# Where the quantised tiles of x are made: beside other stages instead of inside the w2 loops

## The chip, the cores and the metric

The kernel runs on one core of one Trainium2 chip. Its engines are TensorE (PE, with weight loads shown as PEld), VectorE (DVE), ScalarE (ACT), GpSimd (POOL) and SyncE (SP, which here only issues DMAs). Each engine works off its own list of instructions in order and waits where an operand or a buffer is not ready. The metric is the device time of one execution in microseconds.

## The reference

Two layers over x of shape 2 x 4096 x 512, all in float32. What matters here:

```python
xn = _layernorm(x)
x1 = xn @ w1_w.T + w1_b                      # layer 0, "attention": a state-space model
x_conv = _silu(_depthwise_conv(x1, conv_w))  # three taps over the tokens
x_ssm = _ssm(x_conv, A, B_ssm, C_ssm, D_ssm) # a recurrence along 4096 tokens
v = _silu(xn @ v1_w.T + v1_b)
attn = x_ssm * v @ w2_w.T + w2_b
xq, xs = _mx_quantize(xn)                    # layer 0, "ffn": blocks of 32 channels,
wq, ws = _mx_quantize(weight)                # each value to the nearest point of a 6-bit grid
ffn = (xq * xs) @ (wq * ws).T + bias
x = x + attn + ffn
xn = _layernorm(x)                           # layer 1
q, k, v = relu(xn @ Wq.T + bq), relu(xn @ Wk.T + bk), xn @ Wv.T + bv
ctx = (q @ (k^T v)) / (q . sum(k))           # linear attention, 16 heads
y = _layernorm(ctx + xn) * gamma + beta
r, k2 = sigmoid(xr @ W_r.T), square(relu(xk @ W_k.T))   # xr, xk: mixed with the token before
x = x + y + r * (k2 @ W_v.T)
```

`_mx_quantize` takes the largest magnitude of each 32 channels, scales by it and rounds. It needs nothing but the normalised input: it depends on no other part of layer 0.

## The kernel before

The two batches of 4096 tokens are cut into 8 blocks of 512 tokens each (16 blocks, `NK`), and a block into 4 tiles of 128 tokens by 512 channels (`TJ`). The stages follow each other on PE, with the profile's times of each:

- 0 to 451 us, the projections by w1 and v1 of all 16 blocks (`projected`, and `projected_pair` for blocks 13 and 14, with seven products of quarters in place of eight). A block takes 27.5 us. DVE applies the taps (L468), turns the result (L477) and turns the normalised input of the next block into `xnT` (`turned`, L333, two buffers); ACT normalises (L136) and empties the banks (L364, L379).
- 451 to 560 us, the recurrence.
- For batch 0: the w2 loop (`mixed`, 560 to 877 us), the outer sums k^T x (`outer_sums`, 877 to 988), q and W_k by pairs of blocks (`pairs`, 988 to 1192) and the rest of layer 1 (`layer1`, 1192 to 1440).
- For batch 1 the same: 1440 to 1747, 1747 to 1858, 1858 to 2057 and 2057 to 2310 us.

One tile is quantised by `quantised` (L447 to L461), a generator with four steps. It issues the load of the tile from `xi`, the input laid out by blocks of 32 channels (L450, on SP); ACT normalises it in four instructions (L136), DVE finds the largest magnitudes (L187), scales them (L188) and inverts them (L192), and POOL multiplies (L193); DVE rounds (L201) and POOL multiplies back (L202); DVE transposes the tile to its place (L458). The place is a slice of a buffer in SBUF, or a temporary `mx_c` (one buffer), from which SP writes it to `xqd` in DRAM (L460).

Within the w2 loop, block i's product by w2 and by the quantised weight is `x1_by_seven`: DVE makes sums of quarters (L758), PE does seven products (L776), and DVE adds each into x (L794). The first bank is used again by the second product into it, so PE waits for L794. Between products, `gate` prepares the next block's gated input: two loads on SP, a transpose (L621) and a product with v (L622) on DVE. After it comes the product x by Wk of the block before with the key sum on POOL (L848). `tick` is called at fixed points of the loop, and `at` hangs work on a tick: the reading back of x1 (`turned_x1`) and the steps of the tiles to be quantised (L653 to L657), two ticks from tile to tile, four ticks for a tile.

Where the tiles are made before the change: those of blocks 3 to 7 of each batch within its own w2 loop (20 tiles each); blocks 0, 1 and 2 of batch 0 beside the projections, by the table `beside` (L1305); blocks 0 and 1 of batch 1 in `pairs` of batch 0 (`at_pair`, 2 tiles a pair, steps at the start and the middle of a pair) and block 2 in `layer1` of batch 0 (`at_block`). Block 2 of both batches and block 1 of batch 1 go through `xqd` and are read back by `xd_read`, 1 MB each.

In `pairs`, each of the two times seven products of a pair empties its banks by `put_q` (DVE add L1101, ACT L1102) or `put_k` (L1110, then ACT L1111 and L1112), 16 calls a pair; `hold` (L1072, ACT) copies products that are added to later ones; `token_sums` (L1046, DVE) makes the sums `ts` for the next half, `mixed_k` (L1127, L1128) and `mixed_r` (L1137, L1138) the mixed inputs. In `outer_sums`, ACT rescales four tiles of x1 per block, POOL makes the sums `sx` (L927) and DVE the sums `sk` (L935) for the block's seven products on PE (L955); the sums' generator yields once after a block's sums and once after each product.

The order of the instructions on each engine is fixed when the kernel is built: a scheduler places each where its operands and buffers are expected to be ready, and it keeps close to the order in which the program names them.

Of the kernel before, what the change touches and what calls it, by code (L numbers as in the profile page):

```python
# [10 lines left out]
F32 = mybir.dt.float32  # L11
# [6 lines left out]
P = 128  # L18
# [26 lines left out]
def block_kernel(ctx: ExitStack, tc: tile.TileContext, a: dict, out: bass.AP):  # L45
# [400 lines left out]

    def quantised(n, j, dst, temp):  # L447

        xq = yv.tile([P, D], F32, tag="yv", name="xq")
        nc.sync.dma_start(out=xq, in_=a["xi"][n * TJ + j])  # L450
        yield
        laid_normalised(xq, mvi[:, :, n, j, :])
        scales = mx_scaled(xq)
        yield
        mx_rounded(xq, scales)
        yield
        xd = dst().rearrange("p c t -> p (c t)") if dst else temp()
        nc.vector.transpose(xd, xq)  # L458
        if not dst:
            nc.sync.dma_start(out=xqd[n, j], in_=xd)  # L460
        yield  # L461

    def tapped(work, n, x1, cc):
# [160 lines left out]
    def mixed(b, z0, xds, xnTs, mvs, w2, wk, outer):  # L624

        ksum = stay.tile([P, D], F32, tag="ksum", name="ksum", bufs=1)
        zs, xts, pos = {0: z0}, {}, {}
        ahead = len(xds)
        plain = 2 if b == 0 else 1

        def xd_of(m, j):
            if m not in xds:
                xds[m] = t8((P, TJ, CC, P))
            return xds[m][:, j]

# [14 lines left out]
        def at(time, do):  # L650
            events[max(time, clock[0])].append(do)

        for m in range(ahead, NB):  # L653
            for j in range(TJ):
                q = quantised(b * NB + m, j, partial(xd_of, m, j), t2q)
                for step in range(4):
                    at(2 * TJ * (m - 2) + 2 * j - 6 + step, partial(next, q))  # L657

# [191 lines left out]

        if xds[1] is None:
            xd_read(1)
# [12 lines left out]
        for i in range(NB):  # L865
# [13 lines left out]
            if i == 0:  # L879
                first_x1_turned([xn[:, j, :] for j in range(TJ)])  # L880
            xnT = xnTs[i]
            for j in range(TJ):
# [210 lines left out]

    def pairs(b, xnTs, wq, wk, made, kvx, at_pair):

        xks = {}

        def put_q(p, o, n, pm, addend):
            t = t2("q")
            if addend is not None:  # L1100
                nc.vector.tensor_tensor(t, pm, addend, ALU.add)  # L1101
# [12 lines left out]

        def of_q(p):
# [31 lines left out]
        for p in range(NP):  # L1147
            at_pair(p, 0)

# [10 lines left out]
            mixed_r(p)  # L1160
            at_pair(p, 1)

# [83 lines left out]
    with tc.tile_pool(name="tab", bufs=1) as tab:  # L1246
# [3 lines left out]
        with pool("a", 2) as work, pool("pm", 1) as pm:  # L1250
# [46 lines left out]
            def quantise(m, j, dst):  # L1297
# [8 lines left out]
                1: [(0, 0)], 2: [(0, 1)], 3: [(0, 2)], 4: [(0, 3)], 5: [(2, 0)],  # L1306
                9: [(1, 0)], 10: [(1, 1)], 11: [(1, 2)],
                12: [("w", 0), ("w", 1), (1, 3)],
                13: [("w", 2), ("w", 3), (2, 1)],
                14: [(2, 2), (2, 3)],  # L1310
            }
            xd_b1 = None

            def beside_block(n):
                nonlocal xd_b1
                for what, j in beside.get(n, ()):
# [4 lines left out]
                    elif what == 1:  # L1321
                        if xd_b1 is None:
                            xd_b1 = by_tile(single.tile([P, CC * (T + 1)], F32, name="wide"))
                        quantise(1, j, lambda: xd_b1[:, j])
                    else:
                        quantise(2, j, None)

# [61 lines left out]
    for cc in range(CC):  # L1389
        gated(0, 0, z0, cc)  # L1390
    xds = {0: xd0, 1: xd_b1, 2: None}

    for b in range(B):
# [16 lines left out]

        def at_pair(p, half):

            if b + 1 < B:
                for m in range(2):
                    for _ in range(2):
                        next(ahead[m][p])
# [10 lines left out]

        next_in = []
        pairs(b, xnTs, wq, wk1, made, kvx, at_pair)
        layer1(b, xnTs, mvs, kvx, [load_weight(s) for s in ("W_r", "W_v")], at_block)  # L1430
        if b + 1 < B:
            z0, xds = next_in[0], {0: xd0, 1: None, 2: None}
            c_wts = [load_weight("w2_w"), load_weight("Wk")]
# [63 lines left out]
```

## Time and profile before

| | us |
|---|---|
| time, median of 3 runs (lowest, highest) | 2316.46 (2315.31, 2316.96) |
| the profiled execution's own time | 2312.19 |
| its span | 2310.4 |
| PE busy in the span | 2256.2 |
| DVE, ACT, POOL busy | 1615.7, 1024.3, 546.4 |
| HBM traffic | 378.65 MB |

The profile is of one execution. A row of a group names the line, the engine, the operation, output and input, shapes and count; behind the first bar stand the busy time in us and the mean of one in ns, behind the second the engine's idle time just before these instructions and what ended it. A row of waits gives who waited at which line for whom, then us in all, how often, and the longest. In the table by stretches, each engine has its busy time in the stretch and the number of its instructions; PE's granted clock stands as a share of full speed.

### The profile page before, as it was taken

The numbers are of one execution on the slowest core, as the hardware profiler recorded it, in microseconds if no ns is written. First come the engines' busy times: TensorE is split into PE (matmuls) and PEld (weight loads), VectorE is DVE, ScalarE is ACT, GpSimd is POOL, SyncE is SP. The second block draws the span as 40 slices with busy tenths as digits, with TensorE's granted clock in tenths as the row PEclk, the third lists the DMA queues.
The fourth block names the chain that finished last, engine by engine and source line by source line (L and its number), as shares of the span: only waits on it lengthen the run. The fifth ranks groups of instructions, "written<-read, shape, count | busy, mean of one in ns | idle before, by whom it ended". The sixth has DMA issues, their size and how long they took to land. (4 is left out here: it accounts for less than half of the span.)

```text
span 2310.4 us, 24818 instructions
## 1 busy us (share of the span) xinstructions
PE 2256.2 (98%) x7648; PEld 1268.4 (55%) x7648; DVE 1615.7 (70%) x3147; ACT 1024.3 (44%) x2019; POOL 546.4 (24%) x550
## 2 busy tenths in 40 slices
PE   7999999999999899999999999999999999999999
PEld 3444444455476676854445554667676854445554
DVE  6788676665788864376758779688964365667777
ACT  5787674454242333357752222234233246642222
POOL 0011200011445435500021112345434500001111
PEclk9999999999999999999999999999999999999999
DMA  7854542589664556412284435455557312253431
GB/s 249 290 166 139 154 148 108 164 273 330 213 201 153 158 189 209 132 69 110 96 291 155 145 117 185 145 166 190 174 169 223 128 51 96 86 209 146 146 125 58
DMA packets 280725, 378.65 MB, mean 164 GB/s; under 512 B 58256, under 2 KB 119696, under 8 KB 279568
## 3 DMA queue, kind: packets, MB, share of 16 engines
q1 hardware_dynamic: 251504, 309.94, 41.0%
q10 hardware_dynamic: 29088, 67.12, 7.5%
q8 instruction: 61, 1.00, 0.2%
q14 instruction: 72, 0.59, 0.1%
HBM read 238.93 MB, written 138.04 MB: 163 GB/s over the span
## 5 line engine op out<-in xcount | busy, mean ns | idle before, releaser
L1214 POOL TENSOR_TENSOR x<-x,row_beta 128x512 f32<-128x512 f32 x64 | 83.9, 1311 | 591.8 <-ACT xn L136 591.8
L165 PE MATMUL p_acc<-w_W_v,t 128*128 128x512 f32 x512 | 222.3, 592 | 0.0
L165 PE MATMUL p_acc<-w_W_r,xnT 128*128 128x512 f32 x448 | 201.4, 592 | 0.0
L193 POOL TENSOR_TENSOR xq<-xq,mx_rs 128x512 f32<-128x512 f32 x64 | 70.1, 1102 | 404.0 <-DVE mx_rs L192 244.9
L165 PEld LDWEIGHTS p_acc<-w_W_v,t 128*128 128x128 f32 x512 | 97.3, 190 | 122.5 <-issue 119.3
L1220 ACT ACTIVATE r<-p_acc 128x512 f32<-128x512 f32 x64 | 38.2, 597 | 260.6 <-PE p_acc L165 246.5
L136 ACT ACTIVATE xq<-xq,mvi 128x128 f32<-128x128 f32 x256 | 105.9, 483 | 89.1 <-DMA xq<-in_xi 82.5
L848 POOL TENSOR_TENSOR ksum<-ksum,k 128x512 f32<-128x512 f32 x62 | 82.9, 1336 | 205.3 <-ACT k L888 205.2
L776 PE MATMUL p_mm<-w_sums,t 128*128 128x256 f32 x416 | 101.8, 401 | 29.4 <-DVE x L794 29.4
L888 ACT ACTIVATE k<-k 128x512 f32<-128x512 f32 x64 | 40.3, 630 | 202.7 <-DVE k L887 182.4
L468 DVE SCALAR_TENSOR_TENSOR xc<-x,col_conv_w,xc 128x512 f32<-128x512 f32 x128 | 98.1, 787 | 40.0 <-ACT xc L466 21.8
L165 PEld LDWEIGHTS p_acc<-w_W_r,xnT 128*128 128x128 f32 x448 | 80.8, 190 | 80.4 <-issue 80.4
L776 PEld LDWEIGHTS p_mm<-w_sums,t 128*128 128x128 f32 x416 | 83.0, 202 | 45.6 <-DVE x L794 33.5
L165 PE MATMUL p_acc<-xnT,w_w_w 128*128 128x512 f32 x224 | 102.8, 602 | 2.4 <-DVE xnT L333 1.7
L165 PE MATMUL p_acc<-w_Wk,xnT 128*128 128x512 f32 x224 | 100.7, 592 | 0.0
L165 PE MATMUL p_acc<-xnT,w_v_w 128*128 128x512 f32 x224 | 100.7, 592 | 0.0
L165 PE MATMUL p_tr<-w_Wk,xnT 128*128 128x512 f32 x224 | 100.7, 592 | 0.0
L131 DVE BATCH_NORM_STATS2 st<-x 128x6 f32<-128x512 f32 x128 | 84.1, 678 | 22.7 <-DMA x<-in_x 22.0
L1234 DVE TENSOR_TENSOR r<-r,p_acc 128x512 f32<-128x512 f32 x64 | 43.9, 685 | 75.9 <-PE p_acc L165 75.9
L136 ACT ACTIVATE xi<-xi,mvi 128x128 f32<-128x128 f32 x208 | 89.3, 483 | 15.0 <-DMA xi<-in_xi 7.5
L118 ACT ACTIVATE rs_s<-rs_v 128x4 f32<-128x4 f32 (+1 forms) x41 | 8.4, 206 | 196.7 <-DVE rs_v L116 196.6
L776 PE MATMUL p_acc<-w_sums,t 128*128 128x256 f32 x416 | 94.0, 379 | 0.0
(294 smaller groups left out, 4981.8 us busy)
## 6 DMA issues: line engine op xcount, KB each, us to landing
x<-in_x SPq DMA_DIRECT2D x126, 256.0 KB, 5.3
xq<-in_xi SPq DMA_DIRECT2D x64, 256.0 KB, 4.6
vd<-v ACTq DMA_DIRECT2D x64, 256.0 KB, 2.5
cd<-xs SPq DMA_DIRECT2D x64, 256.0 KB, 2.0
xg<-cd SPq DMA_DIRECT2D x16, 1024.0 KB, 7.9
v<-vd SPq DMA_DIRECT2D x64, 256.0 KB, 4.5
xd<-x SPq DMA_DIRECT2D x64, 256.0 KB, 2.3
ktd<-k SPq DMA_DIRECT2D x64, 256.0 KB, 2.2
```

What stands on the lines that cost most here:

```text
L118: nc.scalar.activation(s, v, AF.Sqrt)
L131: nc.vector.bn_stats(st[:, j, :], xt(j))
L136: nc.scalar.activation(dst, src, AF.Identity, bias=mv[:, 0:1], scale=mv[:, 1:2])
L165: nc.tensor.matmul(out_ap, lhsT=lhsT(k), rhs=rhs(k), start=(k == 0), stop=(k == CC - 1))
L193: nc.gpsimd.tensor_tensor(by_block(y), by_block(y), rs.unsqueeze(2).to_broadcast([P, NQ, QB]), ALU.mult)
L468: nc.vector.scalar_tensor_tensor(xc, x1[:, tap : tap + T], conv_w[:, cc, tap : tap + 1], xc, ALU.mult, ALU.add,)
L776: nc.tensor.matmul(po[:, u * 2 * P : (u + 1) * 2 * P], lhsT=x(k)[:, c, u, :], rhs=w(k)[:, c, :], start=first and k == 0 and c == 0 and u == 0,
L848: nc.gpsimd.tensor_tensor(ksum, ksum, kt, ALU.add)
L888: nc.scalar.activation(kt, kt, AF.Relu)
L1214: nc.gpsimd.tensor_tensor(xt[j], xt[j], beta, ALU.add)
L1220: nc.scalar.activation(r, pr, AF.Sigmoid)
L1234: nc.vector.tensor_tensor(rs[j], rs[j], pf, ALU.mult)
```

## The change

All 28 tiles of blocks 1 to 7 of batch 1 and the 24 of blocks 2 to 7 of batch 0 are made outside the w2 loops, written to `xqd`, and read back by `xd_read`, 1 MB per block, two blocks ahead of use, at the start of the product by Wk. Their new places:

- batch 0: blocks 3 to 7 beside blocks 7 to 15 of the projections, in the table `beside`; blocks 0 and 1 stay in SBUF as before;
- batch 1: blocks 6 and 7 in the outer sums of batch 0 (`early`, a step at every second item of the generator, with the tile loaded into a buffer of the pool `t2`), blocks 1 to 5 in the pairs of batch 0 (`later`, a call of `stepped` after each `put_q` and `put_k`), block 0 in `layer1` of batch 0.

`stepped` keeps two tiles under way: each call does the next step of the first, and once that one has done three of its four steps, of the second too, so that a tile takes two calls.

```diff
-    def quantised(n, j, dst, temp):
+    def quantised(n, j, dst, temp, home=None):
-        xq = yv.tile([P, D], F32, tag="yv", name="xq")
+        xq = home("xq") if home else yv.tile([P, D], F32, tag="yv", name="xq")
...
+    done = {}
+
+    def stepped(tiles):
+
+        for tile_steps in tiles[:2]:
+            if tile_steps is tiles[0] or done.get(tiles[0], 0) > 2:
+                next(tile_steps)
+                done[tile_steps] = done.get(tile_steps, 0) + 1
+        while tiles and done.get(tiles[0]) == 4:
+            tiles.pop(0)
...
-        for m in range(ahead, NB):
-            for j in range(TJ):
-                q = quantised(b * NB + m, j, partial(xd_of, m, j), t2q)
-                for step in range(4):
-                    at(2 * TJ * (m - 2) + 2 * j - 6 + step, partial(next, q))
...
+            if 2 < i + 2 < NB:
+                xd_read(i + 2)
             xnT = xnTs[i]
...
             nc.scalar.dma_start(out=qd[b * NB + 2 * p + n, o], in_=t)
+            stepped(later)
...
             nc.scalar.dma_start(out=kd[b * NB + 2 * p + n, o], in_=t)
+            stepped(later)
...
         for p in range(NP):
-            at_pair(p, 0)
...
+        while later:
+            stepped(later)
...
             beside = {
                 1: [(0, 0)], 2: [(0, 1)], 3: [(0, 2)], 4: [(0, 3)], 5: [(2, 0)],
-                9: [(1, 0)], 10: [(1, 1)], 11: [(1, 2)],
-                12: [("w", 0), ("w", 1), (1, 3)],
-                13: [("w", 2), ("w", 3), (2, 1)],
-                14: [(2, 2), (2, 3)],
+                7: [(3, 0), (3, 1)],
+                8: [(3, 2), (3, 3), (4, 0), (4, 1)],
+                9: [(1, 0), (4, 2)],
+                10: [(1, 1), (4, 3), (5, 0), (5, 1)],
+                11: [(1, 2), (5, 2), (5, 3)],
+                12: [("w", 0), ("w", 1), (1, 3), (6, 0), (6, 1)],
+                13: [("w", 2), ("w", 3), (2, 1), (6, 2), (6, 3)],
+                14: [(2, 2), (2, 3), (7, 0), (7, 1)],
+                15: [(7, 2), (7, 3)],
             }
...
-        *_, gt = outer
+        early, later = [], []
+        if b + 1 < B:
+            tile_of = lambda m, j, home=None: quantised((b + 1) * NB + m, j, None, t2q, home)
+            early = [tile_of(m, j, t2) for m in (6, 7) for j in range(TJ)]
+            later = [tile_of(m, j) for m in range(1, 6) for j in range(TJ)]
+        for n, item in enumerate(outer):
+            if n % 2:
+                stepped(early)
+            gt = item
+        while early:
+            stepped(early)
...
             ahead = [
-                [quantised((b + 1) * NB + m, j, None if m else lambda j=j: xd0[j], t2q)
-                 for j in range(TJ)]
-                for m in range(3)
+                quantised((b + 1) * NB, j, lambda j=j: xd0[j], t2q) for j in range(TJ)
             ]
...
                 for _ in range(2):
-                    next(ahead[2][i // 2])
+                    next(ahead[i // 2])
```

More of the change, by code (lines that the diff above doesn't have):

```diff
@@ L627, in mixed @@
         zs, xts, pos = {0: z0}, {}, {}
-        ahead = len(xds)
         plain = 2 if b == 0 else 1
[L631 to L634, printed above, removed]
         def xd_read(m):
@@ L849, in summed @@
             nc.sync.dma_start(out=ktd[b * NB + i, j], in_=kt)
-        if xds[1] is None:
+        if 1 not in xds:
             xd_read(1)
@@ L1092, in seven, with pairs @@
         out(1, 0, p)
-    def pairs(b, xnTs, wq, wk, made, kvx, at_pair):
+    def pairs(b, xnTs, wq, wk, made, kvx, later):
         xks = {}
@@ L1160, in pairs @@
             mixed_r(p)
-            at_pair(p, 1)
             def halfway():
@@ L1325, in beside_block @@
                     else:
-                        quantise(2, j, None)
+                        quantise(what, j, None)
             def scaled(n):
@@ L1390, in block_kernel @@
         gated(0, 0, z0, cc)
-    xds = {0: xd0, 1: xd_b1, 2: None}
+    xds = {0: xd0, 1: xd_b1}
     for b in range(B):
@@ L1405, in block_kernel @@
             ahead = [
-                [quantised((b + 1) * NB + m, j, None if m else lambda j=j: xd0[j], t2q)
-                 for j in range(TJ)]
-                for m in range(3)
-            ]
[L1411 to L1416, printed above, removed]
+                quantised((b + 1) * NB, j, lambda j=j: xd0[j], t2q) for j in range(TJ)
+            ]
         def at_block(i):
@@ L1428, in block_kernel @@
         next_in = []
-        pairs(b, xnTs, wq, wk1, made, kvx, at_pair)
+        pairs(b, xnTs, wq, wk1, made, kvx, later)
         layer1(b, xnTs, mvs, kvx, [load_weight(s) for s in ("W_r", "W_v")], at_block)
         if b + 1 < B:
-            z0, xds = next_in[0], {0: xd0, 1: None, 2: None}
+            z0, xds = next_in[0], {0: xd0}
             c_wts = [load_weight("w2_w"), load_weight("Wk")]
```

## The prediction

> **What bounds the kernel now.** I read the page's first and second parts, then the chain of waits of TensorE (PE), then busy time by stretch, then the timeline of the longest wait.
>
> ```profile
> PE 2256.2 (98%) x7648; PEld 1268.4 (55%) x7648; DVE 1615.7 (70%) x3147; ACT 1024.3 (44%) x2019; POOL 546.4 (24%) x550
> ```
>
> PE is idle for 2310.4 − 2256.2 = 54.2 us. The change leaves PE's instructions as they are, so it can only move that time. PE's waits:
>
> ```profile
> PE p_mm L776 <- DVE x L794: 29.4, 10, 7.2
> PE p_tr L159 <- DVE xn L313: 9.7, 1, 9.7
> PE p_mm L1065 <- DVE q L1101: 3.7, 2, 2.0
> PE p_acc L1065 <- ACT t L1072: 2.9, 2, 2.6
> PE p_acc L165 <- DVE xnT L333: 1.7, 1, 1.7
> ```
>
> The first row is the w2 loop (`x1_by_seven`): the seven products' first bank is taken again only when VectorE (DVE) has added it into x (L794). Measured from start to start of PE's instructions against their own pitch, the lost time is 20.4 us in batch 0 and 11.9 in batch 1, 32.3 together; the rest over 29.4 is matmuls that run longer around the gaps. By stretch (columns: stretch, its length, then PE, PEld, DVE, ACT, POOL busy with counts, PE's granted clock, DMA share, GB/s):
>
> ```profile
> 610.00:657.00 47.00, 39.84 (x143) 28.25 (x142) 37.22 (x61) 18.34 (x46) 26.82 (x24) 0.89 0.49 155
> 783.50:825.40 41.90, 38.18 (x145) 27.29 (x145) 34.88 (x63) 14.36 (x29) 18.08 (x16) 1.00 0.58 189
> 825.40:863.30 37.90, 37.90 (x145) 27.35 (x145) 25.42 (x45) 9.17 (x22) 11.26 (x13) 1.00 0.44 130
> 877.00:988.00 111.00, 111.00 (x482) 91.31 (x481) 46.63 (x57) 36.57 (x61) 60.15 (x66) 1.00 0.48 153
> 1048.00:1096.00 48.00, 48.00 (x113) 21.19 (x112) 32.67 (x54) 34.02 (x60) 4.19 (x4) 1.00 0.28 104
> ```
>
> The third row is the control that the kernel itself holds: a w2 block with no tile to quantise, 37.9 us, PE full. With tiles a block takes 40 to 47 us. The timeline shows why:
>
> ```profile
> 631.66 1.67 POOL L848 TENSOR_TENSOR ksum<-ksum,k 128x512 f32<-128x512 f32 x1 [2.61 <-ACT k L888]
> 633.29 1.04 POOL L193 TENSOR_TENSOR xq<-xq,mx_rs 128x512 f32<-128x512 f32 x1
> 634.37 0.43 DVE L201 TENSOR_SCALAR mx_q<-xq 128x512 fp8e4<-128x512 f32 x1 [2.16 <-POOL xq L193]
> 636.59 0.65 DVE L794 TENSOR_TENSOR x<-x,p_mm 128x512 f32<-128x512 f32 x1
> 637.29 1.22 PE L776 MATMUL p_mm<-w_sums,t 128*128 128x256 f32 x2 [7.16 <-DVE x L794]
> ```
>
> DVE waits for the tile's multiplication on GpSimd (POOL), which stands behind the key sum, which waits for ACT and DVE; the add that PE needs stands behind all of it.
>
> **What is taken out.** 20 tiles per batch leave the w2 loops. By DVE's rows in 610 to 863 us one costs L187 0.66 + L188 0.47 + L192 0.24 + L201 0.85 + L458 0.68 = 2.9 us of DVE, plus POOL 2 x 1.05 and ACT 4 x 0.48 = 1.9. What stays of DVE's work in a block is the control's 25.4 us plus its four missing gates (L621 0.69 + L622 0.82 each, 6.0): 31 of 37.9. What is late next is that add L794 again, if the gates, which move up into the place of the tiles, fill the product phase: I count 15 us of DVE work there in the new order, and the control's phase gave room for 17 to 21. The replacement is one 1 MB read of `xqd` per block on SyncE's queue (SP); page row "xg" has 1 MB landing in 7.9 us, and it is issued about a block (38 us) ahead, behind the last key store. Its cover is that block; without it, 7.9 us per block. In all the kernel gets 40 writes of 256 KB and 10 reads of 1 MB more, 20 MB on 379, in stretches with a DMA share of 0.3 to 0.6. Bounds: 32.3 if all goes; 24 if the 7.7 us of the first block (630 us, beside the largest POOL load) stay. I take **−31**, near the control.
>
> **Projections (up to 451 us): 20 more tiles beside blocks 7 to 15.** PE has no idle time there. In the block from 178.7 us DVE was busy 27.15 of 27.5 us without PE waiting; 265 to 451 shows 14.6 to 20.1 per block. Summing the new order of DVE by the durations of before, between one block's transposes (L333) and the next: for the last five blocks 24, 25, 31, 31, 29 us against pitches of 27.5, 27.5, 27.5, 24.3, 24.3 (before: 20, 13, 18, 17, 29). Sums overstate occupancy by some 10%, but each tile also has two round trips to POOL, about 1.2 us, of which four or five a block are uncovered. Run ahead is not possible, since `xnT` has two buffers. So the transposes for the pair of blocks 13 and 14 end at about 382 to 386 us, where the pair's differences must be ready at 379 to 381. ACT goes from 11 to 21 us in that block, with room. On SP each tile brings a load and a write (0.4 us of issue each), and the write waits for DVE's transpose with `cd` stores and the next block's loads behind it; those loads have a block's lead (27 us). Bounds 0 (round trips covered) and 12 (none is); taken **+5**.
>
> **Outer sums of batch 0 (877 to 988 us): 8 tiles, two per block for four to five blocks.** POOL makes `sx` just in time: the rows L927 of this stretch
>
> ```profile
> L927 POOL TENSOR_TENSOR t<-xg 128x256 f32<-128x256 f32 x28 | 25.8, 942 | 20.3 <-PE p_acc L955 20.3
> L927 POOL TENSOR_TENSOR t<-t,xg 128x256 f32<-128x256 f32 x14 | 11.9, 853 | 0.5
> L927 POOL TENSOR_TENSOR t<-xg,t 128x256 f32<-128x256 f32 x14 | 11.9, 846 | 0.9
> ```
>
> give 49.6 us in seven blocks, 7.1 per block of 12.09, about 4.4 us ahead of PE. Two tiles add 4.2 plus 1.1 for the gaps in which POOL waits for DVE's rounding (0.54 each in the timeline): 12.4 to 13. In the new order four tiles stand between the sums of the third and fourth blocks: 7.1 + 8.4 + 2 = 17.5, 5.4 late, 1 after the lead, and 0.9 per block behind it. ACT's tiles (15 us) and DVE's (23) lie beside 111 us of which they had used 37 and 47. SP issues two loads and two writes more per block, about 2.6 us. Bounds 0 and 15 (an ACT normalisation waits for a late load with the block's rescaling behind it, 3.7 us in each of four blocks); taken **+4**.
>
> **Pairs of batch 0 (1000 to 1192 us): 20 tiles instead of 8, two calls of `put_q`/`put_k` each, so within the first 2.6 pairs.** By the new order DVE has 25.5, 22.1, 20.5, 19.8, 20.5, 17.8 us per half of 24.05, ACT 23.5 at most. The first k half holds about seven tiles in one burst. `mx_c` has one buffer, so a transpose waits for the write before it (2.0 us), and POOL's round trips cost DVE 5.8 + 5.4 us over 9 tiles here, 1.2 per tile (rows from 1000 to 1192 us):
>
> ```profile
> L201 DVE TENSOR_SCALAR mx_q<-xq 128x512 fp8e4<-128x512 f32 x9 | 4.6, 517 | 5.8 <-POOL xq L193 5.8
> L458 DVE STREAM_TRANSPOSE mx_c<-xq 128x512 f32<-128x512 f32 x6 | 4.3, 710 | 6.5 <-POOL xq L202 5.4 <-DMA xqd<-mx_c 1.0
> ```
>
>  20 x 1.2 = 24 over 2.6 pairs (125 us), against 125 − 108 x 0.9 = 28 us of DVE's free time: just covered on the whole, not in the first half. Behind a late DVE stand the adds L1101/L1110 that free PE's banks, and the sums `ts`. Bounds −3 (the 2.6 us wait for ACT at the end, behind a late `xq` load, goes) and 22; taken **+7**.
>
> The Trainium skill bears here. In this trace a DVE subtraction with both inputs in SBUF (L758) takes 677 ns at the median with no POOL arithmetic beside it and 1406 with it, L1046 685 against 1037 in the mean. "SBUF — State Buffer", section "Who interferes with whom", says such an instruction and a POOL instruction that reads SBUF exclude each other for a whole instruction. By the row, 40 POOL multiplications in the pairs add 40 x 0.35 = 14 us to DVE; by the page, up to 40 x 1.05 = 42, an estimate, which would not fit. Neither is in the sum as such; both speak for its upper bound.
>
> Layer 1 has its four tiles in both kernels: 0. The recurrence and batch 1 past its w2 loop lose nothing and gain nothing.
>
> **Sum.** −31 + 5 + 4 + 7 = −15. The profiled execution took 2312.19 (span 2310.4 and 1.79 around it), 4.3 under the runs' median: 2297 in its terms, **2301** against 2316.46.
>
> The clock: the stretch 610 to 657, with the one gap of 7.16 us, was granted 0.89. "TensorE: Matmul & The Clock Gate" (Part 1) says that an idle window of about 3.4 us halves the clock for as long again. By it, four gaps over 3.4 us (7.3, 4.0, 3.9, 3.7 from start to start) cost 1.7 each, 6.8, where the rows show 32.3 − 29.4 = 2.9 over all; so by the page 4 more would come back, and new stalls would pay it too if they are long.
>
> **Rivals.**
> 1. Every cover holds: −29 to −32, 2285 to 2288. For it: 27.15 of 27.5 us of DVE without a stall. Against it: the sums of 31 us in the last projection blocks.
> 2. Slower: the pairs of batch 0 become bound by DVE's own order. The place is the first k half and what follows; the price 108 + 14 (blocked two-input instructions) + 24 (round trips) + 10 (ACT waiting for loads, 2.0 and 3.8 us in two of 9 tiles here) = 156 us against 125, 31 late less some 7 of lead: +24. With +9 from the other two stages: −31 + 24 + 9 = +2, and +10 if the loads are late for most tiles: 2318 to 2327. It decides from 22 us lost in the pairs, 1.1 per tile.
> 3. The w2 loop keeps its stall, because not the tiles but the gates, the key sums or the read of `xqd` hold the add: a saving of 10 instead of 31, with +16: 2322. The control block speaks against it; that it has no gates speaks for it.
> 4. The removed and the new stalls cancel within 4.6 us (0.2%, about what a measurement can tell): 2312 to 2321.
>
> **Chances.** Forecast (2292 to 2311) 0.46, rival 1 0.21, rival 2 0.15, rival 3 0.09, rival 4 0.09; so faster 0.67, same 0.09, slower 0.24. With every bound at its end the sum is 2281 (−32 − 3) or 2341 (−24 + 12 + 15 + 22); the range from 2284 (rival 1) to 2327 (rival 2's upper end) leaves under 2 in 10 out, the most of it above. The likeliest case's own range is 2292 to 2311.
>
> **What would show it.** Right: L776 waits for L794 for less than 4 us, w2 blocks of 38 us with DVE at 31; PE waits for L333 or the pair's differences near 380 us; PE waits at L955 for POOL's `sx` around 920 to 960; L1065 waits for L1101/L1110 near 1000 to 1060. Wrong: idle PE in the projections before 375 us, or over 20 us in the pairs; or w2 blocks still over 40 us.

## The result: slower by 0.4%

The changed kernel takes 2326.44 us (median of 6 runs, 2324.54 to 2327.43) against 2316.71 (6 runs, 2311.24 to 2321.45): a ratio of 1.004, 95% interval 1.0025 to 1.0055. The profiled execution has a span of 2322.8 us against 2310.4. The forecast was 2301 and faster.

TensorE's (PE's) instructions are the same 7648 in both kernels and, but for 16, in the same places of the order. So the place of the time can be found without a model: for each stage, how much longer it takes from its first PE instruction to the first of the next stage than in the profiled execution of before. The boundary at 375 us is put at the last matmul of the plain blocks, so that the pair's first wait counts to the pair.

| stage (times of before) | 0–375 projections, plain | 375–424 the pair of blocks 13, 14 | 560–877 w2 loop, batch 0 | 877–988 outer sums | 988–1192 pairs | 1440–1747 w2 loop, batch 1 | sum |
|---|---|---|---|---|---|---|---|
| after minus before, us | +1.8 | +33.3 | −27.2 | +2.1 | +14.9 | −12.6 | +12.3 |

The profiled execution of before was a quick one: the spans differ by 12.4 us, the medians by 9.7.

The saving came, and more of it than forecast. The loss sits almost wholly in 49 us of the projections and in the pairs. The page's first row and PE's waits (line waited at, who released it, us in all, times, longest):

```profile
PE 2257.0 (97%) x7648; PEld 1266.0 (55%) x7648; DVE 1597.7 (69%) x3147; ACT 1020.7 (44%) x2019; POOL 548.1 (24%) x550
```

```profile
PE p_tr L1066 <- DVE xnT L395: 11.8, 1, 11.8
PE p_tr L159 <- DVE xn L313: 9.6, 1, 9.6
PE p_mm L1066 <- DVE q L1102: 9.0, 2, 7.3
PE p_acc L1066 <- ACT x L364: 8.5, 2, 6.9
PE p_mm L1066 <- ACT v L379: 6.4, 1, 6.4
PE p_acc L1066 <- ACT t L1073: 4.9, 2, 2.7
PE p_acc L1066 <- DVE k L1112: 2.9, 1, 2.9
```

The row of the w2 loop, 29.4 us before, is gone from the list. In its place stand the pair's differences (L395, 11.8 us), the banks of the last plain block, which ACT empties late (L364 and L379, 14.9 us), and q and k in the pairs (L1102, L1112, 11.9 us, of which 1.7 lie in batch 1, as before). By stretch, with the same columns as before:

```profile
341.90:377.00 35.10, 34.30 (x80) 14.70 (x78) 29.11 (x63) 18.23 (x41) 12.47 (x11) 1.00 0.47 165
377.00:412.80 35.80, 11.04 (x16) 3.94 (x16) 33.02 (x66) 17.08 (x41) 17.38 (x15) 0.69 0.46 169
664.40:702.30 37.90, 37.90 (x145) 27.36 (x144) 26.71 (x45) 8.59 (x22) 11.38 (x9) 1.00 0.60 195
888.50:999.50 111.00, 109.66 (x470) 88.53 (x469) 58.24 (x96) 48.93 (x97) 72.48 (x82) 1.00 0.55 188
1020.00:1068.00 48.00, 37.72 (x79) 15.88 (x80) 39.52 (x98) 27.28 (x56) 16.68 (x16) 0.89 0.31 110
```

Third row: a w2 block now takes 37.9 us with PE full, as the control block of before did. Second row: PE works 11 of 35.8 us while VectorE (DVE) is busy for 33 of them, and GpSimd (POOL) has 15 instructions there. The last plain block and the first half of the pair in the kernel before, with PE full and nothing on POOL:

```profile
347.60:375.10 27.50, 27.50 (x66) 12.19 (x65) 14.62 (x30) 9.92 (x22) 0.00 (x0) 1.00 0.35 128
375.10:399.40 24.30, 24.30 (x58) 10.62 (x57) 20.09 (x30) 11.87 (x26) 0.00 (x0) 1.00 0.17 65
```

The timeline of DVE in the changed kernel, at the end of its stretch, shows what PE waited for:

```profile
404.67 0.36 DVE L192 RECIPROCAL mx_rs<-mx_s 128x16 f32<-128x16 f32 x2
406.15 1.59 DVE L201 TENSOR_SCALAR mx_q<-xq 128x512 fp8e4<-128x512 f32 x2 [1.11 <-POOL xq L193]
408.67 0.71 DVE L458 STREAM_TRANSPOSE c<-xq 128x512 f32<-128x512 f32 x1 [0.93 <-POOL xq L202]
409.67 0.71 DVE L458 STREAM_TRANSPOSE c<-xq 128x512 f32<-128x512 f32 x1 [0.29 <-POOL xq L202]
410.31 2.45 DVE L333 STREAM_TRANSPOSE xnT<-xi 128x512 f32<-128x512 f32 x4
```

The transposes of block 14 (L333) end at 412.8 us, in the kernel before at 377.7. Ahead of them on DVE stand seven tiles of the quantiser, with waits for POOL in between.

The rows that answer to those of the outer sums (POOL, 888 to 1000 us) and of the pairs (DVE, 1010 to 1203 us):

```profile
L928 POOL TENSOR_TENSOR t<-xg 128x256 f32<-128x256 f32 x28 | 23.2, 842 | 10.9 <-ACT xg L136 7.0 <-PE p_acc L956 3.9
L928 POOL TENSOR_TENSOR t<-t,xg 128x256 f32<-128x256 f32 x14 | 11.4, 818 | 0.5
L928 POOL TENSOR_TENSOR t<-xg,t 128x256 f32<-128x256 f32 x14 | 11.3, 806 | 0.9
```

```profile
L458 DVE STREAM_TRANSPOSE mx_c<-xq 128x512 f32<-128x512 f32 x16 | 11.2, 702 | 5.2 <-DMA xqd<-mx_c 3.0 <-POOL xq L202 2.2
L201 DVE TENSOR_SCALAR mx_q<-xq 128x512 fp8e4<-128x512 f32 x17 | 10.0, 591 | 10.9 <-POOL xq L193 10.8
```

POOL's slack in the outer sums shrank from 20.3 to 3.9 us of waiting for PE, with 7.0 for ACT beside it, and PE lost 2; what PE waited for there was ACT's rescaling (L136, 1.2 us in two waits), not POOL. In the pairs DVE waits 13.0 us for POOL over 17 tiles, 0.8 each where 1.2 had been counted, and 3.0 for the one buffer `mx_c`.

### The profile page after: what moved, and what is told of

Its sections match the earlier page's. It is cut to its first block, busy times and chain, and to the rows that moved or that the text cites. A ratio compares the mean times of both kernels' runs of the same rounds, so it can differ in the third digit from the quotient of the medians.

```text
span 2322.8 us, 25029 instructions
## 1 busy us (share of the span) xinstructions
PE 2257.0 (97%) x7648; PEld 1266.0 (55%) x7648; DVE 1597.7 (69%) x3147; ACT 1020.7 (44%) x2019; POOL 548.1 (24%) x550
## 4 chain that ended last, share of the span: by engine, by line
PE 49%; DVE 1%; DMA 1%; ACT 0%; issue 0%; POOL 0%; ACTq 0%; POOLq 0%; SPq 0%; DVEq 0%
PE p_acc L165 21%; PE p_mm L1066 4%; PE p_acc L1066 4%; PE p_mm L775 4%; PE p_acc L775 3%; PE p_tr L165 3%; PE p_acc L956 2%; PE p_tr L1066 1%; PE p_mm L1196 1%; PE p_tr L1196 1%; PE p_mm L956 1%; PE p_tr L956 1%; DMA w_W_v<-in_W_v 0%; DMA xq<-in_xi 0%; PE p_acc L733 0%; PE p_mm L733 0%
## 5 line engine op out<-in xcount | busy, mean ns | idle before, releaser
L136 ACT ACTIVATE xq<-xq,mvi 128x128 f32<-128x128 f32 x256 | 108.7, 483 | 31.9 <-DMA xq<-in_xi 21.0
L479 DVE SCALAR_TENSOR_TENSOR xc<-x,col_conv_w,xc 128x512 f32<-128x512 f32 x128 | 103.9, 836 | 27.0 <-ACT xc L477 14.3
L769 POOL TENSOR_TENSOR x<-x,row_w_b 128x512 f32<-128x512 f32 x52 | 72.1, 1409 | 128.9 <-DMA x<-in_x 62.2
L775 PE MATMUL p_mm<-w_sums,t 128*128 128x256 f32 x416 | 94.0, 379 | 0.0
L136 ACT ACTIVATE xi<-xi,mvi 128x128 f32<-128x128 f32 x208 | 89.9, 482 | 9.4 <-DMA xq<-in_xi 2.9
```

Of the source, the lines that this page charges most:

```text
L136: nc.scalar.activation(dst, src, AF.Identity, bias=mv[:, 0:1], scale=mv[:, 1:2])
L479: nc.vector.scalar_tensor_tensor(xc, x1[:, tap : tap + T], conv_w[:, cc, tap : tap + 1], xc, ALU.mult, ALU.add,)
L769: nc.gpsimd.tensor_tensor(xt[:, j, :], xt[:, j, :], b_out, ALU.add)
L775: nc.tensor.matmul(po[:, u * 2 * P : (u + 1) * 2 * P], lhsT=x(k)[:, c, u, :], rhs=w(k)[:, c, :], start=first and k == 0 and c == 0 and u == 0,
```

## The experiments

All kernels below differ by a few lines from the changed kernel or from one another. The table gives the same differences from before by stage (us, profiled executions) and the times; a ratio stands where several executions were timed, the other times are of one. Stages left out did not change by more than 2 us, except where the text says so.

| kernel | projections (0–424) | w2, batch 0 | outer sums | pairs | layer 1 | w2, batch 1 | time | before beside it | ratio |
|---|---|---|---|---|---|---|---|---|---|
| after | +35.2 | −27.2 | +2.1 | +14.9 | 0.0 | −12.6 | 2326.44 | 2316.71 | 1.004 (1.0025–1.0055) |
| b1_only | −2.5 | −2.3 | +2.4 | +15.3 | 0.0 | −12.6 | 2316.03 | 2316.79 | 1.0005 (0.9992–1.0018) |
| b0_only | +36.2 | −27.2 | 0.0 | +1.4 | 0.0 | +2.0 | 2327.21 | 2316.79 | 1.0059 (1.0041–1.0078) |
| b0_two_blocks | +9.1 | −19.2 | +2.2 | +15.8 | 0.0 | −12.6 | 2304.00 | 2316.79 | 0.9944 (0.9928–0.9960) |
| no_pool | +9.9 | −27.2 | +2.4 | +16.8 | 0.0 | −12.6 | 2302.16 | 2316.79 | |
| no_norm | +38.3 | −27.2 | +2.1 | +16.0 | 0.0 | −12.6 | 2329.24 | 2316.74 | |
| three_xnT | +39.3 | −27.2 | +2.2 | +16.8 | 0.0 | −12.6 | 2331.19 | 2316.74 | |
| no_dve | +22.5 | −27.2 | +2.1 | +16.5 | 0.0 | −12.6 | 2313.63 | 2317.16 | |
| loads_two_ahead | +37.8 | −27.2 | +1.9 | +16.2 | 0.0 | −12.6 | 2328.85 | 2322.68 | |
| writes_on_pool | +39.2 | −27.2 | +2.2 | +15.2 | 0.0 | −12.6 | 2329.12 | 2322.68 | |
| all_in_pairs | +3.2 | −19.4 | 0.0 | +12.4 | +0.1 | −12.6 | 2296.52 | 2316.74 | |
| all_in_pairs_timed | +5.7 | −19.4 | 0.0 | +7.9 | −0.1 | −12.6 | 2296.98 | 2314.16 | 0.9928 (0.9911–0.9945) |
| last_in_layer1 | +8.3 | −21.7 | 0.0 | +10.6 | +3.4 | −12.6 | 2296.32 | 2316.74 | 0.9911 (0.9877–0.9945) |
| spread_in_pairs | +6.0 | −19.8 | 0.0 | +1.5 | +11.4 | −12.6 | 2299.23 | 2317.16 | |
| sixteen_in_pairs | +8.8 | −20.0 | 0.0 | −1.6 | +15.5 | −12.6 | 2302.93 | 2317.16 | |
| last_later | +2.0 | −20.0 | 0.0 | +2.2 | +13.5 | −12.6 | 2297.85 | 2322.68 | |
| two_in_loop | +6.3 | −19.7 | 0.0 | −0.3 | +1.1 | −9.5 | 2290.68 | 2314.16 | 0.9898 (0.9881–0.9914) |

How far one execution can be trusted is seen in the table itself: two of one kernel (all_in_pairs and all_in_pairs_timed) differ by 4.5 us in the pairs, and b0_two_blocks and the seven kernels from all_in_pairs down, which have the same tiles in the projections, show +2.0 to +9.1 there. Stages that a kernel leaves alone differ too (b1_only −2.5 and −2.3, b0_only +1.4 and +2.0). For the 4.5 us the traces show the reason. PE's longest waits in the pairs are the same in both executions (2.9, 2.9, 2.6 and 2.4 us), but in one the granted clock falls to one half for 3.4 us behind each of the four, in the other behind one alone; three such drops more are up to 5.1 us of lost work.

### Where the loss sits: one batch at a time

b1_only gives batch 0 back its table and its tiles in the w2 loop; b0_only does that for batch 1.

```diff
+        made_in_loop = (3, 8)[b]            # b1_only; (8, 3)[b] in b0_only
...
+        for m in range(made_in_loop, NB):
+            for j in range(TJ):
+                q = quantised(b * NB + m, j, partial(xd_of, m, j), t2q)
+                for step in range(4):
+                    at(2 * TJ * (m - 2) + 2 * j - 6 + step, partial(next, q))
...
-            if 2 < i + 2 < NB:
+            if 2 < i + 2 < made_in_loop:
                 xd_read(i + 2)
...
```

> Only batch 1's tiles leave their w2 loop (blocks 6 and 7 to the outer sums, 1 to 5 to the pairs of batch 0); batch 0 as before. Theory (the saving in the w2 loops is real, and the loss sits in the projections, where VectorE's own queue delays the turned input of the pair of blocks 13 and 14): no stall at 375 to 425 us, batch 0's w2 loop keeps its 20.4 us, batch 1's loses its 11.9, outer sums +2.3, pairs +5.5; sum -4, a span of about 2306 against 2310.4. Rival (the parts act on each other, by DMA traffic or by the clock): the loss of the changed kernel is not in one place, and this part alone is at or above the time of before.

> Only batch 0's tiles leave their w2 loop, to the projections; batch 1 as before. Theory: -20.4 in batch 0's w2 loop, +35 at the start of the pair of blocks 13 and 14, nothing else: span about 2325, so that this part alone is slower than both kernels. Rival (parts act on each other): the two parts' differences from before do not add up to the +12.4 of the whole within 2 us.

Each part kept its stages' differences to about a microsecond, and the spans add up: +0.2 for b1_only and +12.6 for b0_only against +12.4 for the whole, in part by luck, since untouched stages swing by 2. So no action of the parts on each other shows. The theory's sizes were wrong for batch 1: its w2 loop saves 12.6, but the outer sums and pairs take 17.7 and not 7.8, so that this half of the change gains nothing (1.0005). The 5.5 expected for the pairs fits no count of the trace: in the changed kernel PE's waits in the pairs are 16.8 us against 4.9 before. Batch 0's half is the slower one, by 0.6%, and the projections are its whole loss.

### How many tiles, and which engine's part

b0_two_blocks leaves 8 of the 20 tiles in the projections and returns blocks 5 to 7 to the w2 loop of batch 0.

```diff
+        made_in_loop = (5, 8)[b]
...
-                8: [(3, 2), (3, 3), (4, 0), (4, 1)],
-                9: [(1, 0), (4, 2)],
-                10: [(1, 1), (4, 3), (5, 0), (5, 1)],
-                11: [(1, 2), (5, 2), (5, 3)],
-                12: [("w", 0), ("w", 1), (1, 3), (6, 0), (6, 1)],
...
+                7: [(3, 0), (3, 1)], 8: [(3, 2), (3, 3)],
+                9: [(1, 0), (4, 0)], 10: [(1, 1), (4, 1)], 11: [(1, 2), (4, 2)],
+                12: [("w", 0), ("w", 1), (1, 3)],
```

> Of batch 0 only blocks 3 and 4 (8 tiles) are made beside the projections, none of them beside blocks 12 and 13; blocks 5 to 7 stay in the w2 loop; batch 1 as changed. Theory (VectorE's time before the pair's turned input decides: 12 tiles fewer, each some 2.2 us of work and 1.2 of waits, are 41 us, more than the 35 lost): the stall at 375 to 425 falls to 0 to 4 us; the w2 loop of batch 0 loses the first two stalls (9.9) and keeps 10.5; batch 1 -11.9, outer sums +2.3, pairs +5.5; span 2296 to 2300. Rival (ScalarE's late emptying of the last plain block's banks holds PE, whatever VectorE does): the pair still loses 10 or more; span about 2308.

12 tiles fewer take 26 us off the loss (9.1 left; 5.5 at the pair), and the kernel is faster than before by 0.56%. The w2 loop keeps only 8 us of its wait. The theory's 0 to 4 was too low, the rival's 10 at the pair too high. The 8 tiles that stay are also kept away from blocks 12 and 13, just ahead of the turned input that came late, so this run does not tell their number from their place.

Three kernels then leave out one engine's part of the 20 tiles: no_pool GpSimd's two multiplications, no_norm ScalarE's four normalisations, no_dve VectorE's reductions, rounding and transposes.

```diff
         scales = mx_scaled(xq, part)        # no_pool: mx_scaled and mx_rounded
         mx_rounded(xq, scales, part)        # return before their nc.gpsimd.tensor_tensor
...
+        if part != "no_norm":
             laid_normalised(xq, mvi[:, :, n, j, :])
...
+        if part:                            # no_dve: by ones, and no transpose
...
+            for _ in range(2):
+                nc.gpsimd.tensor_tensor(by_block(xq), by_block(xq), ..., ALU.mult)
...
+            nc.sync.dma_start(out=xqd[n, j], in_=xq)
...
```

> The changed kernel without GpSimd's two multiplications in the 20 tiles of batch 0's blocks 3 to 7 (they are left out, so those tiles are not scaled); all else of the tiles stays. Theory (work and waits of VectorE add up before the pair): in 274 to 413 us its waits for GpSimd are 12.4 us and the lengthened instructions beside GpSimd another 12; without them the loss at 375 to 425 falls from 35 to about 11. Rival (VectorE's own instructions alone decide, the waits were slack): it stays at 25 or more. Second rival (GpSimd is the cause altogether): it falls under 3.

> The changed kernel without ScalarE's four normalisations in the 20 tiles of batch 0's blocks 3 to 7 (left out, so those tiles are quantised as they were loaded); all else stays. Theory (VectorE's work and waits before the pair's turned input add up): its waits for ScalarE at the tiles' first step (L187) are 11 us of the 138 between 274 and 413 us, so the loss at 375 to 424 falls from 33 to about 22. Rival (ScalarE, late with the banks of the last plain block, is itself what holds PE: 15 of PE's waits there name it): it falls to 15 or less.

> The changed kernel without VectorE's part in the 20 tiles of batch 0's blocks 3 to 7 (largest magnitudes, scales, rounding and transposes are left out; loads, ScalarE's normalisations, GpSimd's two multiplications, by ones, and the writes stay). Theory (what lacks in the projections is time on VectorE, its work and its waits): 20 times 2.2 us of work and 1.2 of waits are gone, and the loss of 35 at 11 to 424 us falls to 0 to 4. Rival (GpSimd's instructions, which lengthen VectorE's taps beside them, or the extra loads and writes carry it): 10 or more stay.

no_pool fell as the theory said, to 9.9, and block 14's transposes end at 387.3 us. Groups on DVE between 200 and 425 us, first of the changed kernel:

```profile
L479 DVE SCALAR_TENSOR_TENSOR xc<-x,col_conv_w,xc 128x512 f32<-128x512 f32 x60 | 51.1, 878 | 12.0 <-ACT xc L477 7.8 <-ACT x L346 3.7
L201 DVE TENSOR_SCALAR mx_q<-xq 128x512 fp8e4<-128x512 f32 x24 | 14.0, 588 | 10.7 <-POOL xq L193 10.7
```

then of no_pool, whose lines are numbered two and four higher:

```profile
L483 DVE SCALAR_TENSOR_TENSOR xc<-x,col_conv_w,xc 128x512 f32<-128x512 f32 x68 | 49.7, 753 | 12.7 <-ACT xc L481 8.4 <-ACT x L350 3.7
L203 DVE TENSOR_SCALAR mx_q<-xq 128x512 fp8e4<-128x512 f32 x23 | 10.1, 448 | 4.6 <-POOL xq L195 4.6
```

The taps, DVE instructions with two inputs in SBUF, go back from 878 to 753 ns, and this wait for POOL falls from 10.7 to 4.6 us. That fits what the Trainium skill says ("SBUF — State Buffer", section "Who interferes with whom": such an instruction and a GpSimd instruction that reads SBUF keep each other out). No run here separates that lengthening from the waits.

The other two went against the theory. Without ScalarE's part, the loss stays (38.3): it only moves ahead, 18.1 us of it now before 375 us. Without VectorE's part 22.5 stay, where 0 to 4 had been expected, and block 14's transposes still end at 398.5 us. PE's largest wait there (L364, 9.5 us in two) comes from a new thing, on ACT:

```profile
379.37 1.65 ACT L136 ACTIVATE xq<-xq,mvi 128x128 f32<-128x128 f32 x4 [10.47 <-DMA xq<-in_xi]
380.92 0.67 ACT L364 ACTIVATE x<-p_acc,col_w_b 128x512 f32<-128x512 f32 x1
```

ACT waits 10.5 us for a tile that SyncE loads late, and the bank that PE needs (L364) stands behind. So the theory that VectorE's time alone, work and waits added, decides the loss falls: of the three engines' parts, GpSimd's is the one whose removal brings most back (25 of 35), VectorE's brings 13, ScalarE's nothing. Each of the three is one execution, and each removal also changes what the scheduler puts where and what the queues wait for.

### Order, loads and writes

Three kernels keep all the work and move it: a third buffer for xnT, so that block 14's transposes may be placed earlier; the tiles' loads issued two tiles ahead; the tiles' writes issued from GpSimd's queue.

```diff
-        xnT = work.tile([P, CC, T], F32, tag="xnT", name="xnT")
+        xnT = work.tile([P, CC, T], F32, tag="xnT", name="xnT", bufs=3)    # three_xnT
...
+                next(q)                                                    # loads_two_ahead
+                loaded.append(q)
+                finish_tiles(2)                        # all steps of all but the last two
...
-            nc.sync.dma_start(out=xqd[n, j], in_=xd)
+            (nc.gpsimd if n < NB and n > 2 else nc.sync).dma_start(out=xqd[n, j], in_=xd)   # writes_on_pool
```

> The changed kernel with three buffers for the turned input xnT in the projections, in place of two; the work is the same. Theory (in the order on VectorE, the transposes of block 14 stand behind the tiles because with two buffers they could not be placed before block 12 was done; in time VectorE then runs behind that order): with a third buffer they stand earlier and the pair loses under 10 instead of 33. Rival (VectorE has more to do before the pair than time, whatever the order): 20 or more stay.

> The changed kernel, with the load of each tile beside the projections issued two tiles ahead of its other steps (the work is the same). Theory (a tile's load stands on SyncE's queue behind the write of the tile before, which waits for VectorE; ScalarE then waits in order for the load with the banks behind it, and VectorE for ScalarE, so that each tile passes all queues one after the other): the loss of 35 at 11 to 424 us falls to 20 or less. Rival (what lacks is the engines' time, of which GpSimd's multiplications and what they lengthen are 25): 30 or more stay.

> The changed kernel, with the 20 writes of batch 0's tiles issued from GpSimd's queue instead of SyncE's, where they wait for VectorE's transposes for 47 us between 200 and 430 us with other loads and stores behind them. Theory (SyncE's queue, blocked by these writes, is what couples the tiles): the loss falls to 20 or less. Rival (SyncE's waits are slack): 30 or more stay.

All three went to the rivals: 39.3, 37.8 and 39.2 us. With the third buffer block 14's transposes end at 399.6 us instead of 412.8, but the plain blocks before them now lose 23.8 us, because ACT empties their banks late (waits at L364 and L379). In these kernels the order changes where PE waits; what it loses stays within about 4 us of the changed kernel's.

### The pairs and the tiles of the outer sums

The next kernels start from b0_two_blocks and move batch 1's tiles. In all_in_pairs all 28 tiles of blocks 1 to 7 stand in the pairs and none in the outer sums; in last_in_layer1 blocks 6 and 7 stand in layer 1.

```diff
-            early = [tile_of(m, j, t2) for m in (6, 7) for j in range(TJ)]
-            later = [tile_of(m, j) for m in range(1, 6) for j in range(TJ)]
+            later = [tile_of(m, j) for m in range(1, 8) for j in range(TJ)]    # all_in_pairs
...
+            last = [tile_of(m, j) for m in (6, 7) for j in range(TJ)]          # last_in_layer1
...
                     next(ahead[i // 2])
+                    if last:
+                        stepped(last)
...
```

> As b0_two_blocks, but batch 1's blocks 6 and 7 are made in the pairs of batch 0 too, behind blocks 1 to 5 (28 tiles in 56 of the 64 calls), none in the outer sums. Theory (the 15 us lost in the pairs come mostly from the last tiles of the outer sums, which stand on VectorE before the sums that end that stage and so make it 9 to 10 us late into the pairs): outer sums lose 0, the first q half goes back to the 2 us of before, the pairs lose 4 to 9 in all. Rival (VectorE's free time in the pairs is what lacks): with 8 more tiles there they lose 20 or more.

> As b0_two_blocks, but batch 1's blocks 6 and 7 are made in layer 1 of batch 0 (one tile a block, where VectorE has 24 of 31 us busy and ScalarE 8), none in the outer sums. Theory: outer sums 0 instead of +2.2, pairs +4 to +7 instead of +15.8, layer 1 0 to +3; about 10 us under b0_two_blocks, so a span of 2293 to 2299. Rival (the pairs' loss is that of their own 20 tiles): no gain in the pairs, span 2303 or more.

> The kernel of all_in_pairs again, timed in three rounds beside the kernel before: 2294 to 2300 against 2316, ratio 0.990 to 0.995.

With no tile called for in the outer sums (the scheduler still places the first four of the pairs' tiles there), those lose nothing, and the pairs lose 8 to 12 instead of 15, although all_in_pairs puts 8 tiles more into them; the longest wait for q falls from 7.3 us to 2.9 and 3.0. So the last tiles of the outer sums did cost time at the start of the pairs: in the changed kernel four of them stand on DVE between 984 and 1006 us, ahead of the sums that end that stage (L973 to L979), which end at 1007.9 us; PE is 10.5 us behind the kernel before at that point, these sums 19.2. But the larger part of the pairs' loss stayed, against the theory's 4 to 9 (all_in_pairs: 12.4 and 7.9 in two executions) and 4 to 7 (last_in_layer1, 10.6).

spread_in_pairs steps after two of every three calls, so that 20 tiles last through all four pairs; sixteen_in_pairs after every second, with 16 tiles, the rest in layer 1; last_later begins layer 1's tiles with its third block.

```diff
+        def step_later():
+            if later and puts[0] % 3 < 2:       # puts[0] % 2 in sixteen_in_pairs
+                stepped(later)
+            puts[0] += 1
...
+                for _ in range(3 if i > 1 else 0):    # last_later; range(3) in sixteen_in_pairs
+                    if last:
+                        stepped(last)
...
```

> As last_in_layer1, but a step of the 20 tiles in the pairs is taken after two of every three calls of put_q and put_k, so that they last through all four pairs instead of 2.6. Theory (the 10.6 us lost in the pairs come from their density in the first halves): 3 to 6 remain. Rival (each tile costs its waits wherever it stands): 9 or more remain.

> As last_in_layer1, but only 16 tiles (blocks 1 to 4) stand in the pairs, a step after every second call, and 12 (blocks 5 to 7) in layer 1 with block 0's four. Theory: the pairs lose 1 to 4 instead of 10.6, layer 1 4 to 8 instead of 3.4; in all 3 to 8 under last_in_layer1. Rival (layer 1 has no free time for more than its eight): layer 1 loses 10 or more.

> As spread_in_pairs, but the 8 tiles in layer 1 begin with its third block. Theory (the 11.4 us lost at layer 1's start come from the last tiles of the pairs and the first of layer 1 meeting there): layer 1 loses 0 to 4, all else as spread_in_pairs, so 7 to 11 under it, a span of 2286 to 2291. Rival (they come from the tail of the pairs alone): 8 or more stay in layer 1.

Spread out, the 20 tiles cost the pairs 1.5 us. But 11 to 15 us appeared at the start of layer 1 (PE waiting at L1214 for the denominators on DVE): pairs and layer 1 together lose 12.9 in spread_in_pairs and lost 14.0 in last_in_layer1, so spreading alone moved the loss and won nothing clear of one execution's swing. The loss also stays when the tiles of layer 1 are called for later (13.5): ACT normalises the last of them at 1240 us and PE begins the third block at 1243, so the program's order does not keep the scheduler from placing them early. two_in_loop takes those 8 tiles out of layer 1 and makes them in batch 1's w2 loop, as before the change.

```diff
-        made_in_loop = (5, 8)[b]
+        made_in_loop = (5, 6)[b]
...
-            last = [tile_of(m, j) for m in (6, 7) for j in range(TJ)]
+            last = []
```

> As spread_in_pairs, but batch 1's blocks 6 and 7 are made in its own w2 loop as before the change, so that layer 1 of batch 0 holds only block 0's four tiles, as in both kernels. Theory (the loss that wandered from the pairs to layer 1's start comes from those 8 tiles meeting the tail of the 20): layer 1 back to 0 to 2, pairs +1.5, and batch 1's w2 loop saves 6 to 8 instead of 12.6; span 2287 to 2292. Rival (the tail of the 20 tiles alone makes the loss at layer 1's start): 8 or more stay there and the span is 2300 or more.

The loss at layer 1 goes (+1.1), the pairs stay at −0.3, and batch 1's w2 loop still saves 9.5. So it is the 8 tiles fewer, with the rest spread, that took the loss away. This kernel is faster than the one before and the changed one: 2290.68 us, ratio 0.9898 to before (0.9881 to 0.9914). PE's longest waits in it, but for 9.6 us at the kernel's start:

```profile
PE p_mm L788 <- DVE x L806: 7.7, 4, 4.1
PE p_mm L1079 <- DVE q L1120: 3.8, 2, 2.0
PE p_mm L1079 <- ACT t L1086: 2.6, 1, 2.6
```

The first row is the w2 loop's add (L794 before): 7.7 us in place of 29.4, with the tiles of 5 of the 10 blocks moved out of the loops.

## Why the prediction was wrong

**What is taken out: −31, measured −39.8.** The mechanism was right: the wait for the add in the w2 loop went, and a block takes 37.9 us, the control's time; DVE is busy 26.7 of it, less than the 31 counted. The size was off, beyond its bound of −32.3, because that sum held only gaps of over a quarter of a microsecond on PE, not the matmuls that ran longer behind them; the sentence that the change can only move PE's 54.2 us of idle time left them out too. In the kernel before the clock granted was down there (last three columns: clock, DMA share, GB/s):

```profile
625.00:645.00 20.00, 12.84 (x48) 10.57 (x47) 14.79 (x25) 10.77 (x27) 7.29 (x7) 0.74 0.62 189
710.00:730.00 20.00, 17.97 (x74) 14.82 (x73) 15.81 (x25) 10.95 (x27) 4.19 (x4) 0.91 0.67 205
750.00:775.00 25.00, 21.21 (x80) 16.64 (x79) 19.97 (x32) 13.30 (x32) 5.97 (x6) 0.86 0.70 222
```

and 1.00 in the same blocks after. Cut finer, the trace of before has the clock at 0.50 for 10.2 us from 632.3, for 3.4 us from 721.0 and for 6.8 us from 762.0, and at full speed in the rest of both w2 loops. PE works for 13.8 of these 20.5 us; half of that, 6.9, is nearly all of 39.8 − 32.3 = 7.5. The Trainium skill's rule ("TensorE: Matmul & The Clock Gate", Part 1) agrees with the halving and with lengths in multiples of 3.4 us. But that it made 6.8 us of four gaps is luck: only the first two of them (7.3 and 4.0 us from start to start) were followed by a drop, and so was one of 2.2 us, which is under its 3.4. These sums hold for this execution of before: b1_only runs the same loop of batch 0 in 2.3 us less, and b0_only that of batch 1 in 2.0 more, 1.7 of them by one drop behind a gap of 3.2 us that brought none in the kernel before.

**Projections: +5, bounds 0 and 12, measured +35.** This is the step that failed: "So the transposes for the pair of blocks 13 and 14 end at about 382 to 386 us". They end at 412.8. Its dates follow from DVE's sums of four blocks, 24 + 25 + 31 + 31 = 111, behind the transposes of block 10, which end at 274.4 us in the changed kernel. From there on DVE's instructions occupy 109.8 us, as counted; but 28.5 us of waits lie between them. Most stand at two lines (rows from 274 to 413 us):

```profile
L187 DVE TENSOR_REDUCE mx_s<-xq 128x16 f32<-128x512 f32 x19 | 12.5, 665 | 11.0 <-ACT xq L136 11.0
L201 DVE TENSOR_SCALAR mx_q<-xq 128x512 fp8e4<-128x512 f32 x19 | 11.9, 634 | 8.3 <-POOL xq L193 8.3
```

The others are for POOL at L458 and for the taps' part on ACT. The prediction had priced the waits for POOL in the sentence before (about 1.2 us, four or five uncovered per block: 19 to 24 us over four blocks, or half of that if 1.2 us is meant for both round trips of a tile) and then let the sums' overstatement of 10% pay for them; the wait for ACT's normalisation it put at nothing, "with room". But the sums overstated hardly anything: 109.8 + 28.5 = 138, and 274.4 + 138 = 412. And the bound for "none is covered" does not follow from its own numbers: 385 us and 19 to 24 more are 23 to 30 behind 379 to 381, not 12. The runs also show that the account by DVE alone is too simple: without DVE's part of the tiles 22 us stay, and without ACT's, 38.

**Outer sums: +4, measured +2.1.** Near in size, but the wait is another: POOL's `sx` was to hold PE, and PE waited for ACT's rescaling instead, which the prediction had only in its upper bound. **Pairs: +7, bounds −3 and 22, measured +14.9.** Within the bounds, twice the value taken. The burst in the first k half was there (a wait of 2.9 at L1112 and the slower clock behind it, 4.9 us together). What was not in the sum is that the last tiles of the outer sums hold DVE at the start of the pairs, which goes with the 7.3 us at L1102 (2.9 and 3.0 without them). **Layer 1 and the rest: 0**, measured 0.

**The rivals.** Rival 2, slower by DVE's own order, named the right mechanism (waits for POOL, lengthened two-input instructions, ACT waiting for loads), but for the pairs; it happened in the projections. That its time (2318 to 2327, measured 2326) holds is luck: it is made of −31, +24 in the pairs, +9 in the other two stages and up to +10 for late loads, and the stages measured −39.8, +14.9 and +37.3. The projections' row of 27.15 busy us in a block of 27.5 without a stall had been taken as a reason to think that DVE can be filled there. That block has four POOL instructions; the stretches of 35 us that lost have eleven and fifteen. Their number alone does not decide, though: the block from 265 us of the kernel before has eleven too, with DVE busy for 18.71 us and PE full. Rivals 1, 3 and 4 did not occur: the w2 loop's wait went as a whole.

**What stays open.** The loss in the projections is shown to be the 20 tiles' (b1_only), to be 2 to 9 us with 8 tiles and 35 with 20 (the 8 also stand elsewhere), and to hang most on GpSimd's multiplications, in one execution of each kernel without an engine's part. Which chain of in-order queues sets its size is not settled: VectorE's time alone, the order at the pair, the place of the loads and that of the writes were each tried and are not it by themselves.

## What to carry to other kernels

An engine that is busy two thirds of a stage (DVE for 151 of the 225 us from 200 to 425 in the kernel before) has not the last third free for work that passes through other engines: each hand-over in an in-order queue is a wait, so set the new work's own waits beside its durations and add both up to the date at which the first consumer needs the last result. When work is moved out of a stalled loop, move only as much as each place takes: 8 tiles beside the projections and 20 spread thinly through the pairs gave 1%, all of them gave a loss. And price a gap on TensorE by the whole stage's length against a stage without gaps, since the matmuls behind a gap can run slower too; take such a length from more than one execution.

## What the runs showed of the hardware

- Behind gaps on TensorE the granted clock fell to 0.50 for 3.4, 6.8, 10.2, 13.7 or 20.5 us. In the 18 traces, past the first 50 us, every gap of over 3.8 us in the list of waits was followed by such a drop. Gaps of 2.0 to 3.8 us brought one or not, the same gap in two executions too (2.9 us in all_in_pairs).
- A tap on VectorE with both inputs in SBUF took 878 ns on the mean with the tiles' GpSimd multiplications beside it, 753 without them.
- The same instructions in the same order differ between two executions: 4.5 us in one stage of 200 us (all_in_pairs), where the clock fell four times in one and once in the other.
